# Moving the weighted values ahead of the mixing and projection steps inside each attention unit

## The chip, the cores and the metric

The kernel runs on one core of one Trainium2 chip. The metric is device microseconds of one execution, the median of several executions. A profile is one further execution, recorded by the hardware profiler. PE is the matrix engine (TensorE), with PEld its weight loads, DVE is VectorE, ACT is ScalarE, POOL is GpSimd, and SP issues most of the DMAs.

## The reference, cut to what matters

A gated transformer block on 32 sequences of 128 tokens with 128 features, everything in float32:

```
x = x + tanh(g_xattn) * xattn(layernorm(x), ctx)
x = x + tanh(g_ffn)   * ffn(layernorm(x))

xattn(x, xa):   q, k, v    = x  @ Wqkv + bqkv           16 heads of 8 features
                _, ka, va  = xa @ Wqkv_aux + bqkv_aux
                main = softmax(q k^T / sqrt(8)) v
                aux  = softmax(q ka^T / sqrt(8)) va
                out  = main * (1 - sigmoid(g)) + aux * sigmoid(g)
                return out @ Wo + bo

ffn(x):         64 experts of width 64, 8 of them for each token, out of 4 of 8 groups,
                plus one shared expert; weights are normalised sigmoid scores times 2.5
```

## The kernel before, in words

**Units.** Attention is done in 64 units: unit u is sequence b = u // 2 with kind = u % 2, kind 0 being the main attention (keys and values from x) and kind 1 the one on the context. All 16 heads of a unit are done together, as 4 groups of 32 rows of the matrix array (two heads' rows and a row that holds a constant, padded to 32).

**Steps of a unit**, each with its own function and its tiles, named as in the profile:

- `scores_max(u)`: PE computes the scores `sp` (L554, 16 matmuls on 32-row tiles of the array), DVE takes the negated maxima `nm` (L563).
- `queries(u)`: PE transposes the maxima into `nt` (L580, full array), DVE adds them to the block-wise queries and writes `qa` (L582), so that the second pass of the scores comes out with the maximum already subtracted.
- `softmax(u)`: PE computes the scores again, transposed, as `st` (L600, 32-row tiles), ACT takes the exponential into two tiles `pt` (L610).
- `values(u)`: PE multiplies `pt` with the values into `op` (L623, 32 matmuls on 32-column tiles of the array), ACT copies it to `osb` (L632). The value tile carries a column of ones, so that the sums come with it.

**Steps of a sequence**, after its second unit, in the generator `output(b, osb)`, which stops twice: `divide` transposes `osb` into `ot` (L639) and DVE divides (`rd` L642, `at` L644); `mix` adds the two kinds of attention on PE with two matmuls against the identity into `mt` (L656) and ACT copies to `msb` (L660); `project` multiplies by Wo into `yp` (L666), DVE adds it to x (L667) and takes the statistics of the second layernorm (L222).

**Steps of the next pair of sequences**, in the generator `prepare(a)`, one piece at a time: statistics, normalising on POOL, transposes `tp` (L293), projections `pp` in three pieces (L305; ACT adds the bias into `qk`, L321, and half of the masked copies `bd`, L266; POOL does the other half, L268), and the values `vp` (L349; ACT copies them with L359).

**Experts.** From the middle of attention on, groups of 128 tokens that `route` has sorted by expert group are run in between: `pair` issues gate and up products `gu` (L1026, full array, with `begin_tiles` and its transposes `xq..t`, L1004, where a new set of rows begins), `add_up` the turn `ht` (L1041) and the down product `y` (L1054; ACT scales it with L1061). When attention is over, the rest of the experts runs alone.

**Order.** The order on PE, ACT, DVE and POOL is the order of the calls: nothing is rescheduled. The loop runs over u from 0 to 68 and works on three units at a time. In iteration u, with k = u % 4:

1. `queries(u-1)`, `scores_max(u)`;
2. the first `turn`: expert products `gu`, if there are any;
3. for even k one step of `outputs` (this is `mix`), for odd k one step of `steps` (`pp` for k = 1, `vp` for k = 3);
4. `values(u-2)`, then `softmax(u-1)`;
5. in turns `add_up`, another step of `outputs` (`project` for even k, `divide` for odd k), another step of `steps`, routing.

**Banks.** Two PSUM pools serve this loop. `banks` ("s", three buffers of two banks) holds `sp`, `st`, `gu`, `ht` and the routing tiles. `bank` ("m", two buffers of one bank) holds `nt`, `mt`, `pp`, `vp`, `op`, `y`, `ot`, `yp`, `tp`, which take the two buffers in turn, so that a tile waits until the last but one before it has been read.

Of the kernel before, what the change touches and what calls it, by code (L numbers as in the profile page):

```python
# [51 lines left out]
def gated_block_kernel(  # L52
# [41 lines left out]
    def bank(name):  # L94
        return ps_m[-1].tile([P, 512], F32, tag="m", name=name)
# [155 lines left out]
    def clear_values(n):  # L251
        k = follow(nc.gpsimd.memset(vpads[n], 0.0), "POOL")
        tc.add_manual_dep(k.ins, cleared.ins.name, BEHIND)
        tv = vpads[n].rearrange("p k i g (r j) e -> p (k i g r) j e", j=2)
        for j in range(2):
            nc.gpsimd.memset(tv[:, :, j, MX + j : MX + j + 1], 1.0)
# [280 lines left out]
    def unit_parts(u):  # L537
        b, kind = divmod(u, 2)
        a, i = divmod(b, AG)
        qkk, vs, bds = parts[a]  # L540
        return b, kind, i, qkk[0], qkk[1 + kind], vs[:, kind], bds[0], bds[1 + kind]
# [32 lines left out]
    def queries(u):  # L574

        b, kind, i, q, k, v, qbd, kbd = unit_parts(u)
        nm = nm_of.pop(u)
        nt = bank(f"nt{u}")
        for n in range(4):
            nc.tensor.transpose(nt[:, ts(n, S)], nm[:, n].rearrange("p g e -> p (g e)"), ident)  # L580
        qa = work.tile([P, 2, 2, S], F32, tag="qa", name=f"qa{u}")
        V.tensor_tensor(  # L582
            qa,
            nt.rearrange("p (r j s) -> p r j s", r=2, j=2),
            qbd[:, :, :, ts(i, S)],
            ALU.add,
        )
        qa_of[u] = qa
# [26 lines left out]
    def values(u):  # L615

        b, kind, i, q, k, v, qbd, kbd = unit_parts(u)
        pt = p_of.pop(u)
        op = bank(f"op{u}").rearrange("p (n s) -> p n s", s=S)
        for r in range(2):  # L620
            for j in range(2):
                for g in range(4):
                    nc.tensor.matmul(  # L623
                        op[g * SLOT : (g + 1) * SLOT, r],
                        v[:, i, g, 2 * r + j, :],
                        pt[g // 2][:, g % 2, 2 * r + j, :],
                        start=j == 0,
                        stop=j == 1,
                    )
        if kind == 0:  # L630
            osb_of[b] = work.tile([P, 4, S], F32, tag="osb", name=f"osb{b}", bufs=1)
        nc.scalar.copy(osb_of[b][:, 2 * kind : 2 * kind + 2, :], op[:, 0:2])  # L632
        return osb_of.pop(b) if kind else None

    def divide(b, osb):

        ot = bank(f"ot{b}")
        for n in range(4):
            nc.tensor.transpose(ot[:, ts(n, S)], osb[:, n, :], ident)  # L639
        oh = ot.rearrange("p (n e) -> p n e", e=SLOT)  # L640
        rd = work.tile([P, H, 2], F32, tag="rd", name=f"rd{b}")
        V.reciprocal(rd, oh[:, :, MX : MX + 2])  # L642
        at = work.tile([P, H, 2, DH], F32, tag="at", name=f"at{b}", bufs=1)
        V.tensor_tensor(  # L644
            at,
            oh[:, :, 0:MX].rearrange("p n (j e) -> p n j e", e=DH),
            rd.unsqueeze(3).to_broadcast([P, H, 2, DH]),
            ALU.mult,
        )
        return at.rearrange("p n j e -> p (n j e)")  # L650

    def mix(b, af):

        mt = bank(f"mt{b}")
        for kind in range(2):
            nc.tensor.matmul(  # L656
                mt[:, 0:S], af[:, ts(kind, D)], ident, start=kind == 0, stop=kind == 1
            )
        msb = work.tile([P, S], F32, tag="msb", name=f"msb{b}")
        nc.scalar.copy(msb, mt[:, 0:S])  # L660
        return msb

    def project(b, msb):
        bg, i = divmod(b, BG)
        yp = bank(f"yp{b}")
        nc.tensor.matmul(yp[:, 0:D], msb, wo_sb, start=True, stop=True)  # L666
        V.tensor_tensor(x_sb[bg][:, i, :], yp[:, 0:D], x_sb[bg][:, i, :], ALU.add)  # L667
        ln_stats(x_sb[bg][:, i, :], mv2[bg][:, i, :])
# [8 lines left out]
    def scatter_some(n):  # L677

        for _ in range(min(n, len(to_scatter))):
            f, *a = to_scatter.pop(0)  # L680
            f(*a)
# [397 lines left out]
    def gather_some(n):  # L1079

        while to_gather and n:
            n -= 1
            f = to_gather.pop(0)
            while f and not f():
                f = to_gather.pop(0) if to_gather else None
# [96 lines left out]
    def round_begins():  # L1182

        nonlocal clock
        clock += 1
        if routed in (sum(ROUNDS[: c + 1]) for c in range(len(ROUNDS))):
            scatter_some(1)
        for c in range(len(ROUNDS)):
            if routed < sum(ROUNDS[: c + 1]) or to_scatter and c not in begun:
                continue  # L1190
            at = clock - begun.setdefault(c, clock)
            if at == 1:
                load_rows_of(c, 0)
            elif at >= (3 if alone else 6) and c not in started and len(parts_of) < 2:
                begin_tiles(c, 0)
                load_rows_of(c, 1)
                started[c] = clock
# [8 lines left out]
    def pair():  # L1206

        nonlocal fresh
        if todo and ready(todo[0]):
            kind, *job = todo.pop(0)  # L1210
            fresh = True
            if kind == "all":
                waiting.append((job, hidden(*job)))
            else:
                waiting.append((job, group_hidden(*job)))
                c, q, n = job
                if n == 0 and q + 1 < NQ[c]:
                    begin_tiles(c, q + 1)
                    load_rows_of(c, q + 2)
# [22 lines left out]
    NU = 2 * B  # L1242
# [23 lines left out]
    def output(b, osb):  # L1266

        at = divide(b, osb)
        yield
        msb = mix(b, at)  # L1270
        yield
        project(b, msb)
        if b % BG == BG - 1:
            routing.append(route(b // BG))

    def more(it):
        next(it, None)
# [27 lines left out]
    def turn(there):  # L1305

        if there:
            pair()
        round_begins()
        scatter_some(1)  # L1310
        gather_some(1)

    for u in range(NU + 5):
        if 10 <= u:
            for k in islice(clear, 1):
                tc.add_manual_dep(k.ins, reached[min(u, NU) - 1], AFTER)
        if 1 <= u <= len(weight_loads):
            for k in weight_loads[u - 1]():
                tc.add_manual_dep(k.ins, reached[u - 1], AFTER)
        if 0 <= u - 1 < NU:  # L1320
            queries(u - 1)
        if u == 0:
            first, steps = steps, prepare(1)
            more(steps)
            more(steps)
        if u < NU:
            scores_max(u)
        if u == 0:
            finish_gates()
            more(first)  # L1330
            ictx.close()
            rt = ctx.enter_context(tc.tile_pool(name="rt", bufs=1))
            hp = ctx.enter_context(tc.tile_pool(name="hp", bufs=2))
            clear_values(1)
            count_tables()
            nc.gpsimd.memset(lower, 1.0)
            nc.gpsimd.affine_select(
                out=lower,
                in_=lower,
                compare_op=ALU.is_gt,  # L1340
                fill=0.0,
                base=0,
                pattern=[[1, NG], [-1, NG]],
                channel_multiplier=0,
            )
        k = u % UA
        n = plan(u)

        turn(n > 0)
        if k % 2 == 0:  # L1350
            more(outputs)
        else:
            more(steps)
        osb = values(u - 2) if 0 <= u - 2 < NU else None
        if osb is not None:
            finished = output((u - 2) // 2, osb)
        if 0 <= u - 1 < NU:
            softmax(u - 1)
        add_up()
        copy_some()  # L1360
        if osb is not None:
            outputs = finished
        route_some(1)
        turn(n > 1)
        more(outputs)
        copy_some()
        route_some(2)
        add_up()
        turn(n > 2)
        if u:  # L1370
            more(steps)
        route_some(1)
        add_up()
        if k == 2 and u < NU - UA - 2:
            coming = prepare((u + 2) // UA + 1)
            more(coming)
        elif k == 3:
            more(coming)
            steps, coming = coming, iter(())
        use_bank()  # L1380
        turn(False)
        copy_some()
# [67 lines left out]
```

## Time and profile before

| | us |
|---|---|
| median of 7 executions | 1046.16 |
| lowest and highest | 1043.49, 1047.85 |
| the profiled execution, time | 1047.54 |
| the profiled execution, span | 1045.8 |

| engine | busy us | share of the span |
|---|---|---|
| PE | 942.6 | 90% |
| PEld | 638.1 | 61% |
| DVE | 608.5 | 58% |
| POOL | 539.4 | 52% |
| ACT | 494.9 | 47% |

| stretch of the span, us | what runs | PE busy us | granted PE clock |
|---|---|---|---|
| 30 to 110 | attention alone | 77.28 | 1.00 |
| 110 to 300 | attention, routing and scatters | 163.84 of 190 | 0.94 |
| 300 to 340 | the last scatters of the first round, first expert rows | 32.43 of 40 | 0.83 |
| 340 to 560 | attention with experts in between | 201.73 of 220 | 1.00 |
| 560 to 700 | experts, second round of routing | 123.84 of 140 | 0.96 |
| 700 to 950 | experts alone | 245.92 of 250 | 0.99 |
| 950 to 1046 | the last sequences through all experts, gathers | 76.00 of 96 | 0.92 |

The span is what the profiler saw of the execution; 1.74 us of the execution's own time lie around it. Busy time counts matmuls as they are issued and modelled, so the starts of neighbouring instructions tell more about the price of a step than their durations do. The granted clock is the share of full speed at which the matrix array was allowed to run.

### The profile page before, as it was taken

What the parts mean: (1) busy time and instruction counts of PE and PEld (TensorE: products, weight loads), DVE (VectorE), ACT (ScalarE), POOL (GpSimd) and SP (SyncE); (2) the same over time, 40 slices, a digit from 0 to 9 for tenths busy, and PEclk for the clock granted to TensorE, in tenths of its full rate; (3) what the DMA queues carried; (4) which work ended last, traced back from release to release, by engine and by line L of the source; (5) the groups of instructions that cost most, each with busy time, mean ns of one, the idle gap of its engine ahead of it and who ended that gap; (6) DMA issues with size and microseconds to landing.
All of it is one profiled execution on the core that took longest, in us unless ns stands there. A gap on an engine that the chain in (4) does not pass through costs nothing.

```text
span 1045.8 us, 20766 instructions
## 1 busy us (share of the span) xinstructions
PE 942.6 (90%) x7704; PEld 638.1 (61%) x7704; DVE 608.5 (58%) x1248; ACT 494.9 (47%) x943; POOL 539.4 (52%) x867
## 2 busy tenths in 40 slices
PE   6999789789897889989999799998999999999876
PEld 5777566566674566666666466665667666764332
DVE  5576875766763765575666374553455555546453
ACT  2566555454554445455544344544555555542111
POOL 3435378587676365855753767511333332007770
PEclk8999999898997999999999899999999999999989
DMA  5544234101011000100120122244222222115530
GB/s 140 141 119 144 92 131 149 41 29 44 7 42 55 22 17 24 61 19 27 39 63 12 55 81 75 78 110 110 78 84 76 76 76 69 41 50 141 141 86 25
DMA packets 100007, 75.19 MB, mean 72 GB/s; under 512 B 23942, under 2 KB 92166, under 8 KB 99910
## 3 DMA queue, kind: packets, MB, share of 16 engines
q1 hardware_dynamic: 90662, 55.11, 18.7%
q0 software_dynamic: 8960, 18.36, 5.6%
q8 instruction: 65, 1.06, 0.4%
q10 hardware_dynamic: 288, 0.39, 0.1%
q14 instruction: 32, 0.26, 0.1%
HBM read 39.63 MB, written 34.21 MB: 71 GB/s over the span
## 4 chain that ended last, share of the span: by engine, by line
PE 53%; POOL 20%; DVE 13%; issue 6%; DMA 4%; ACT 3%; SPq 1%; POOLq 0%; ACTq 0%; DVEq 0%
PE gu L1026 16%; PE y L1054 9%; POOL xslot L869 6%; POOL yg L1095 5%; PE st L600 5%; PE op L623 4%; PE ht L1041 4%; PE sp L554 3%; DVE nm L563 3%; PE pp L305 2%; POOL bd L268 2%; PE gu L970 2%; PE nt L580 2%; POOL row L234 1%; DMA xq<-xslot 1%
## 5 line engine op out<-in xcount | busy, mean ns | idle before, releaser
L954 DVE TENSOR_TENSOR th<-gu,th 128x512 f32<-128x512 f32 x158 | 108.9, 689 | 158.6 <-ACT th L947 157.0
L947 ACT ACTIVATE th<-gu 128x512 f32<-128x512 f32 (+1 forms) x132 | 78.9, 597 | 194.7 <-PE gu L1026 106.2
L563 DVE TENSOR_REDUCE nm<-sp 128x8 f32<-128x1024 f32 x128 | 150.7, 1219 | 17.2 <-PE sp L554 16.9
L1054 PEld LDWEIGHTS y<-wd_sb,hT 128*128 128x128 f32 x1008 | 130.3, 194 | 47.3 <-issue 45.7
L610 ACT ACTIVATE pt<-st 128x1024 f32<-128x1024 f32 x128 | 124.1, 1021 | 50.4 <-PE st L600 50.4
L1054 PE MATMUL y<-wd_sb,hT 128*128 x1008 | 136.8, 279 | 0.9 <-ACT hT L1043 0.9
L1026 PE MATMUL gu<-wg_sb,xqT 128*128 x252 | 133.2, 611 | 3.3 <-DVE th L954 2.7
L1095 POOL DMA_INDIRECT yg<-yslot,place x112 | 110.7, 988 | 43.4 <-issue 30.9
L1026 PE MATMUL gu<-wu_sb,xqT 128*128 x252 | 129.6, 596 | 0.0
L869 POOL DMA_INDIRECT xslot<-row,place x112 | 114.6, 1024 | 22.0 <-issue 21.0
L268 POOL TENSOR_SCALAR bd<-qk,mask 128x256 f32<-128x256 f32 x90 | 82.7, 930 | 45.1 <-ACT qk L321 44.4
L623 PE MATMUL op<-pt,v 128*32 128x128 f32 x2048 | 73.2, 286 | 24.8 <-DVE qa L582 24.3
L1006 POOL TENSOR_TENSOR wg<-xq,mine 128x256 f32<-128x256 f32 x32 | 24.6, 770 | 135.0 <-DMA xq<-xslot 134.9
L1026 PEld LDWEIGHTS gu<-wu_sb,xqT 128*128 128x128 f32 x252 | 48.2, 191 | 61.1 <-issue 61.1
L600 PE MATMUL st<-qa,qk 32*128 32x256 f32 x1024 | 82.8, 415 | 2.5 <-DVE nm L563 2.1
L554 PE MATMUL sp<-bd,qk 32*128 32x256 f32 x1024 | 80.1, 416 | 3.8 <-DVE qk L319 3.8
L1043 ACT COPY hT<-ht 128x512 f32<-128x512 f32 x126 | 74.1, 588 | 12.2 <-PE ht L1041 0.9
L623 PEld LDWEIGHTS op<-pt,v 128*32 128x32 f32 x2048 | 54.8, 114 | 39.7 <-DVE qa L582 29.3
L1041 PE MATMUL ht<-ident,h 128*128 128x128 f32 x504 | 76.1, 274 | 0.2 <-DVE th L954 0.2
L956 DVE TENSOR_TENSOR h<-th,wq 128x512 f32<-128x512 f32 x98 | 69.5, 710 | 3.3
L958 POOL TENSOR_TENSOR h<-th,wq 128x512 f32<-128x512 f32 x28 | 29.2, 1043 | 77.4 <-DVE th L954 61.1
L1061 ACT ACTIVATE yo<-y,tgf 128x128 f32<-128x128 f32 x126 | 46.4, 368 | 41.6 <-PE y L1054 33.4
(278 smaller groups left out, 1492.1 us busy)
## 6 DMA issues: line engine op xcount, KB each, us to landing
xslot<-zero SPq DMA_DIRECT2D x16, 768.0 KB, 3.8
xq<-xslot SPq DMA_DIRECT2D x32, 384.0 KB, 3.3
yslot<-yo SPq DMA_DIRECT2D x32, 256.0 KB, 2.3
cw<-w_dram SPq DMA_DIRECT2D x32, 256.0 KB, 4.0
x<-in_x_dram SPq DMA_DIRECT2D x16, 128.0 KB, 3.1
ctx<-in_ctx_dram SPq DMA_DIRECT2D x16, 128.0 KB, 2.6
wg_sb<-in_L_ffn_We_gate_dram SPq DMA_DIRECT2D x8, 256.0 KB, 3.5
wu_sb<-in_L_ffn_We_up_dram SPq DMA_DIRECT2D x8, 256.0 KB, 3.8
```

The source lines that it names most:

```text
L268: nc.gpsimd.tensor_scalar(bd[:, r, j, :], qk[:, r], mask[:, j : j + 1], None, ALU.mult)
L554: mm = nc.tensor.matmul(sp[g // 2][:, g % 2, 2 * r : 2 * r + 2, :], q[p0 : p0 + SLOT, r, ts(i, S)], kbd[p0 : p0 + SLOT, r, :, ts(i, S)], s ...
L563: V.tensor_reduce(nm[:, :, 2 * gp : 2 * gp + 2, MX].rearrange("p b g -> p g b"), sp[gp], AX.X, ALU.max, negate=True,)
L600: nc.tensor.matmul(st[g // 2][:, g % 2, 2 * r : 2 * r + 2, :], k[p0 : p0 + SLOT, r, ts(i, S)], qa[p0 : p0 + SLOT, r], start=True, stop=True,)
L610: nc.scalar.activation(pt, st[gp], AF.Exp, scale=1.0 / math.sqrt(DH))
L623: nc.tensor.matmul(op[g * SLOT : (g + 1) * SLOT, r], v[:, i, g, 2 * r + j, :], pt[g // 2][:, g % 2, 2 * r + j, :], start=j == 0, stop=j == 1,)
L869: k = nc.gpsimd.indirect_dma_start(out=xslot[c], out_offset=IndirectOffsetOnAxis(ap=place[c][:, i0 + i, r : r + 1], axis=0), in_=row[:, i, :],
L954: V.tensor_tensor(th[0:m], gu[0:m, 1], th[0:m], ALU.mult)
L1026: nc.tensor.matmul(gu[:, i], xt[:, ts(n, P)], w[:, ds(v[n], 1), :].rearrange("p o f -> p (o f)"), start=True, stop=True,)
L1041: nc.tensor.transpose(ht[:, 0, ts(p, P)], h[:, ts(p, P)], ident)
L1054: nc.tensor.matmul(y[:, 0:D], hs[:, ts(p, P)], w[:, ds(v[n], 1), p, :].rearrange("p o d -> p (o d)"), start=p == 0, stop=p == GP - 1,)
L1095: nc.gpsimd.indirect_dma_start(out=k["yg"][:, n, r, :], out_offset=None, in_=yslot[c], in_offset=IndirectOffsetOnAxis(ap=place[c][:, 2 * k ...
```

## The change

In each iteration of the loop, step 4's `values(u-2)` is called ahead of step 3 in place of behind it: the products with the values come directly behind the scores (and behind expert products, where there are any), and `mix`, `pp` or `vp` follows them. The generator `output(...)` is made at the same place as before relative to `values`; it is still handed to `outputs` only further down, so the step of `outputs` that is called here is the same one as before. Nothing else is changed, and no instruction is added or removed.

```diff
         n = plan(u)
 
         turn(n > 0)
+        osb = values(u - 2) if 0 <= u - 2 < NU else None
+        if osb is not None:
+            finished = output((u - 2) // 2, osb)
         if k % 2 == 0:
             more(outputs)
         else:
             more(steps)
-        osb = values(u - 2) if 0 <= u - 2 < NU else None
-        if osb is not None:
-            finished = output((u - 2) // 2, osb)
         if 0 <= u - 1 < NU:
             softmax(u - 1)
```

On PE the order of a unit changes from `nt sp [gu] mt|pp|vp op st` to `nt sp [gu] op mt|pp|vp st`. On ACT the copy to `osb` comes ahead of `msb`, `qk` or the values' copies; the exponentials stay behind both. The order of operations on DVE, POOL and SP stays as it was. The bank that `op` takes is now the one that was last used before `nt`, and `mt`, `pp` or `vp` takes the one of `nt`.

## Prediction

> **What bounds the kernel now.** I read the page first, then PE's timeline unit by unit, then the chain of work that ended last, in its order of time. The page says that PE is busy 90% of the span, and that the chain runs through PE for 53%, POOL 20%, DVE 13%.
>
> ```profile
> PE 942.6 (90%) x7704; PEld 638.1 (61%) x7704; DVE 608.5 (58%) x1248; ACT 494.9 (47%) x943; POOL 539.4 (52%) x867
> ...
> PE 53%; POOL 20%; DVE 13%; issue 6%; DMA 4%; ACT 3%; SPq 1%; POOLq 0%; ACTq 0%; DVEq 0%
> ...
> L623 PE MATMUL op<-pt,v 128*32 128x128 f32 x2048 | 73.2, 286 | 24.8 <-DVE qa L582 24.3
> ```
>
> The last line is the moved step, `op`: 24.3 us of PE's idle time stand in front of it, ended by DVE's `qa`. `op` does not read `qa`; it takes the bank that `nt` had, and `qa` is what reads `nt`. From the timeline, a unit without experts, one with experts, and three places where `op` has other neighbours (start, duration, in us):
>
> ```profile
> 138.30 1.15 PE L554 MATMUL sp<-bd,qk 32*128 32x256 f32 x16
> 139.37 0.71 PE L656 MATMUL mt<-ident,at 128*128 128x128 f32 x4
> 140.02 1.08 PE L623 MATMUL op<-pt,v 128*32 128x128 f32 x32
> 141.03 1.15 PE L600 MATMUL st<-qa,qk 32*128 32x256 f32 x16
> 142.10 0.49 PE L666 MATMUL yp<-wo_sb,msb 128*128 128x128 f32 x2
> ...
> 390.95 1.02 PE L1026 MATMUL gu<-wu_sb,xqT 128*128 x2
> 391.81 0.61 PE L656 MATMUL mt<-ident,at 128*128 128x128 f32 x4
> 392.34 1.08 PE L623 MATMUL op<-pt,v 128*32 128x128 f32 x32
> 393.36 1.15 PE L600 MATMUL st<-qa,qk 32*128 32x256 f32 x16
> 394.43 1.16 PE L1054 MATMUL y<-wd_sb,hT 128*128 x8
> 395.43 0.60 PE L1041 MATMUL ht<-ident,h 128*128 128x128 f32 x4
> ```
>
> ```profile
> 34.84 1.15 PE L554 MATMUL sp<-bd,qk 32*128 32x256 f32 x16
> 35.91 1.08 PE L623 MATMUL op<-pt,v 128*32 128x128 f32 x32
> ...
> 549.31 1.02 PE L1026 MATMUL gu<-wu_sb,xqT 128*128 x2
> 550.27 1.08 PE L623 MATMUL op<-pt,v 128*32 128x128 f32 x32
> ...
> 564.37 1.08 PE L623 MATMUL op<-pt,v 128*32 128x128 f32 x32
> 565.38 1.16 PE L1054 MATMUL y<-wd_sb,hT 128*128 x8
> 566.37 0.60 PE L1041 MATMUL ht<-ident,h 128*128 128x128 f32 x4
> ```
>
> The reader is to take differences of starts. The array is used in three shapes: rows (`sp`, `st`: 32*128), full (128*128), columns (`op`: 128*32). Where the shape changes, a step takes longer. `mt` takes 0.65 between rows and columns (139.37 to 140.02; 0.64 in most units), and 0.53 where a full-shape `gu` stands before it (391.81 to 392.34). `gu` takes 0.86 before `mt` and 0.96 before `op`. `y` takes 1.00 behind `st` and 0.99 behind `op`, against 0.89 where the experts run alone (575.65 to 576.54 in the timeline). So leaving a shape costs about 0.1 us and entering one another 0.1.
>
> **The change, part by part.** The same instructions run; what moves is the order and the banks. There are 64 `op` steps; in four (u = 2, 61, 63 and 65) nothing stands between, so 60 pairs are swapped: 39 without an expert product or expert transposes in between, 21 with.
>
> *39 pairs without experts: nothing.* Before: rows, full, columns, rows; after: rows, columns, full, rows; three changes of shape each way. For `mt`, before: 1.07 + 0.64 + 1.01 = 2.72 from `sp` to `st`. After: `sp` to `op` 1.07 (at 34.84), `op` to a full step 1.01 (at 564.37), and `mt` between columns and rows, which the trace does not show. It is at most the 0.64 between rows and columns, at least the 0.53 that `nt` takes before `sp` with a full step ahead of it. I take 0.64, as `y` pays the same behind `op` as behind `st`: 2.72, a difference of 0 (bounds -0.11 to 0). `pp` and `vp` go the same way.
>
> *21 pairs with experts: one change more.* Before: rows, full `gu`, full `mt`, columns, rows; three changes. After: rows, full `gu`, columns, full `mt`, rows; four. Before, from the second `gu` to `st`: 0.86 + 0.53 + 1.01 = 2.40. After: 0.96 + 1.01 + 0.64 = 2.61, with 0.53 for the last 2.50. The price is 0.10 to 0.21, and I take 0.20. The Trainium skill has a rule that speaks against this change: "TensorEngine Tiling (Array Packing)", Key Properties, says that a change of tiling mode, not of tile alone, drains the engine. It gives no time; "TensorE: Matmul & The Clock Gate" (Part 2) gives some 128 cycles for a wavefront to leave, an estimate of 0.05 us at the 2.4 GHz it states, by which one more change would cost about 1.1 us over 21 pairs.
>
> Not all 21 pay at the end. In the chain of waits, `mt|vp|pp` and `op` stand next to each other in 12 of them: at 330, 341, 383, 392, 412, 423, 432, 468, 477, 487, 508 and 520 us. In the others the chain goes through something else: the second half of `st` waits for DVE's `nm` (371, 401, 456, 497; the like at 360), or the chain leaves PE at `gu` for ACT, DVE and POOL (353, 445, 542). These I cost at nothing; if that cover goes, each is 0.2. At 330 the array runs at half clock (`op` 1.87), so 0.35. At 558 (u = 64) `op` waits for `msb`; after, `mt` waits for `osb`, and `st` comes about 0.2 later. Sum: 11 x 0.20 + 0.35 + 0.20 = 2.75 us later.
>
> *The waits for `qa`.* `op` no longer waits for it, but `mt`, `pp` or `vp` does, as it takes `nt`'s bank, and `st` does, which reads it. So what runs behind the wait is `mt` (0.64) in place of `op` (1.01): 0.37 less in even iterations; in odd ones `pp` 1.06 or `vp` 1.08: 0.05 to 0.07 more. There are 14 waits. At 119 and 148 the chain goes on through POOL, at 127, 197, 265 and in the four expert units through DVE's `nm`: nothing. At 188 the wait of 6.05 is followed by half clock and then by `yp`, on which DVE waits:
>
> ```profile
> 181.47 0.71 PE L656 MATMUL mt<-ident,at 128*128 128x128 f32 x4
> 188.24 1.93 PE L623 MATMUL op<-pt,v 128*32 128x128 f32 x32 [6.05 <-DVE qa L582]
> 190.10 2.09 PE L600 MATMUL st<-qa,qk 32*128 32x256 f32 x16
> ```
>
> `op` took 1.86 there; a cold `mt` takes 1.15 (at 249.91): 0.71 gained. At 218 (wait 3.39) the clock comes back before `yp`: 0.38 gained. At 133, 258 and 272: 0.05, 0.05 and 0.07 lost; at 286 cold `pp` against cold `op`: nothing. Together 0.92 gained.
>
> *ACT and what else is moved.* `msb` comes a step later, behind `osb` (0.37): it is ready about 0.4 us after `st` starts, and `yp` follows 1.08 after that start. `qk` (0.84) now runs while `st` does: it ends about 0.95 after `pp`, the exponentials start 1.18 after it; 0.2 are left. `osb` is earlier, so `ot` has more room. `op` now needs both exponentials at the place where `mt` stood. In the units that follow `vp`, `mt` starts only 0.20 after the second exponential ends (70.63 against 70.43), and PE starts 0.04 after a releaser (ACT's `qk`, 202.72 to 202.76): nothing. POOL's `bd` gets its `qk` 1 us later at k = 1; the copy is used three units later. If the covers on ACT went, 0.2 in some ten units would be 2 us.
>
> *Sum.* 2.75 - 0.92 = +1.8 us. The profiled execution took 1047.54 (span 1045.8), which becomes 1049.4; it stands 1.4 above the median of 1046.16, so the median becomes 1048.0.
>
> **The rivals.**
>
> *Faster, through the clock.* After waits of 6.05 (188), 3.39 (218) and 2.73 us (286) the array runs at half clock; the granted clock is 0.58 from 186 to 196. After 2.63 (127) and 2.11 (148) it does not. After the move the idle times are 5.7, 3.0 and 2.8, hardly shorter. If the clock holds all the same, `op`, `st` and their followers cost 2.9, 1.4 and 1.5 less. With 0.38 for each of two waits in place of 1.09, and 0.17 lost, that is 2.75 + 0.17 - 0.76 - 5.8 = -3.6: 1042.5. It decides from two of the three spells on. Against it: a wait of 1.62 (245) was followed by a cold spell and the same wait at 348 was not, so length alone does not set it. The Trainium skill's "TensorE: Matmul & The Clock Gate" (Part 1) puts the idle time that throttles at about 3.4 us; by it only the spell at 218 would go, and the sum would be about +0.4. This trace has one behind 2.73.
>
> *Slower by more.* All 21 expert pairs pay because the covers are thinner than the chain shows, and the waits give nothing: 19 x 0.20 + 0.35 + 0.20 + 0.17 = +4.5: 1050.7. A cold spell more (1.4 to 2.9) comes to the same. For it: the covers by `nm` are 0.4 us waits (`st` at 374, 404, 458, 500). Against it: a wait that DVE ends does not move with PE.
>
> *No change.* The later PE meets the waits for POOL's scatters (5.95 at 580, 3.49 at 317) and is swallowed: 1046.2. Against it: in both places the chain comes from PE shortly before.
>
> *The change does not do what it says* is no case here: the order after it shows `op` behind `sp` or `gu` in all 60.
>
> **How the numbers follow.** Forecast +1.8: 0.48. Slower by more: 0.20. No change: 0.18. Faster: 0.14. The range reaches from 1042.8 (the faster case; the lower bounds of the shape costs, 39 x -0.11 = -4.3, end in the same place) to 1051.5 (the slower case and some spread of the median). The likeliest case alone, with the price from 0.10 to 0.21 and 1 us of spread, is 1046.0 to 1049.5. About 0.2%, 2.1 us, is what a measurement can tell from no change, so the forecast lies close to that edge: I give half of it to each side. Slower by more than that: 0.24 + 0.19 = 0.43; faster: 0.14 and a little of the others, 0.16; within: 0.41.
>
> **What would show it.** Right: `op` at about 0.96 behind `gu` and `mt` at 1.01 behind `op` in the units from 340 to 560 us, from `gu` to `st` 2.6 in place of 2.4; units before 300 unchanged where nothing waits; the 24.3 us in front of `op` gone from it and found, slightly less, in front of `mt`, `pp`, `vp`. Wrong: `st` or `mt` starting earlier relative to `qa` than 0.6, cold spells missing or added, `op` waiting for ACT's exponentials, `yp` for `msb`.

## The result and the profile after

The changed kernel takes 1054.84 us (median of 17 runs, 1051.43 to 1058.57) against 1046.21 (44 runs of the kernel before, 1042.71 to 1049.87). The ratio is 1.0082, with a 95% interval from 1.0072 to 1.0093: 8.6 us slower, outside the predicted range. The profiled execution has a span of 1054.0 (before 1045.8).

The page of the changed kernel: busy times, the shares of the chain that ended last, and the group of the moved step.

```profile
PE 950.7 (90%) x7704; PEld 640.4 (61%) x7704; DVE 608.4 (58%) x1248; ACT 495.9 (47%) x943; POOL 540.7 (51%) x867
...
PE 53%; POOL 22%; DVE 11%; issue 6%; DMA 4%; ACT 3%; SPq 1%; POOLq 0%; ACTq 0%; DVEq 0%
...
L623 PE MATMUL op<-pt,v 128*32 128x128 f32 x2048 | 70.9, 280 | 1.3 <-ACT qk L321 1.1
```

The list of PE's waits (total us, times, longest) says where the 24.3 us went that stood in front of `op`:

```profile
PE mt L656 <- DVE qa L582: 13.8, 5, 5.7
...
PE pp L305 <- DVE qa L582: 5.7, 3, 2.4
...
PE vp L349 <- DVE qa L582: 3.6, 2, 2.2
```

Together 23.1 us: moved, and slightly less, as forecast. A unit with experts, from the timeline after:

```profile
395.51 1.02 PE L1026 MATMUL gu<-wu_sb,xqT 128*128 x2
396.46 1.08 PE L623 MATMUL op<-pt,v 128*32 128x128 f32 x32
397.47 0.71 PE L656 MATMUL mt<-ident,at 128*128 128x128 f32 x4
398.11 1.15 PE L600 MATMUL st<-qa,qk 32*128 32x256 f32 x16
```

Differences of starts: 0.95, 1.01, 0.64, so 2.60 from `gu` to `st`; 2.61 was forecast, 2.40 stood before. To see where time is lost, I subtract, for each unit, the start of its `nt` before from the one after, and look at how that shift steps from unit to unit. From unit 2 to unit 15 each step is at most 0.01 us. From there to 262 us there are steps both ways, up to 2.5 us, where the array waits or changes its clock; in all the shift goes from -1.33 at unit 15 to -0.19 at 262.04. In most of the expert units it steps by 0.17 to 0.21. The largest step is elsewhere: +3.95 between the `nt` at 262.04 and the one at 268.52 us (times of before), ahead of the first expert. There the prediction had 0.05 to 0.07 us for a wait, and nothing else.

The timeline before at that place (start, duration, engine, what it does, the wait in front of it and who ended it):

```profile
257.52 0.84 ACT L321 ACTIVATE qk<-pp,bcol 128x256 f32<-128x256 f32 x2 [1.22 <-PE pp L305]
258.11 1.83 POOL L268 TENSOR_SCALAR bd<-qk,mask 128x256 f32<-128x256 f32 x2 [2.90 <-ACT qk L321]
259.91 0.72 POOL L761 TENSOR_TENSOR eq<-eq,lower 128x256 f32<-128x256 f32 x1
260.71 0.73 POOL L762 TENSOR_TENSOR gt<-gt,eq 128x256 f32<-128x256 f32 x1
261.81 0.41 DVE L766 TENSOR_REDUCE gm<-gt 128x32 f32<-128x256 f32 x1
262.26 0.18 DVE L767 TENSOR_SCALAR gm<-gm 128x32 f32<-128x32 f32 x1
...
264.40 0.68 DVE L582 TENSOR_TENSOR qa<-nt,bd 128x512 f32<-128x512 f32 x1
265.14 1.08 PE L623 MATMUL op<-pt,v 128*32 128x128 f32 x32 [0.47 <-DVE qa L582]
266.15 1.25 PE L600 MATMUL st<-qa,qk 32*128 32x256 f32 x16
```

And after:

```profile
258.00 1.13 PE L305 MATMUL pp<-srcT,wpad 128*128 128x256 f32 x4 [2.32 <-DVE qa L582]
259.17 0.84 ACT L321 ACTIVATE qk<-pp,bcol 128x256 f32<-128x256 f32 x2 [3.05 <-PE pp L305]
259.75 1.83 POOL L268 TENSOR_SCALAR bd<-qk,mask 128x256 f32<-128x256 f32 x2 [3.77 <-ACT qk L321]
261.55 0.72 POOL L761 TENSOR_TENSOR eq<-eq,lower 128x256 f32<-128x256 f32 x1
262.35 0.72 POOL L762 TENSOR_TENSOR gt<-gt,eq 128x256 f32<-128x256 f32 x1
263.11 0.42 DVE L766 TENSOR_REDUCE gm<-gt 128x32 f32<-128x256 f32 x1 [1.41 <-POOL gt L762]
263.56 0.43 DVE L767 TENSOR_SCALAR gm<-gm 128x32 f32<-128x32 f32 x1
...
266.11 0.68 DVE L582 TENSOR_TENSOR qa<-nt,bd 128x512 f32<-128x512 f32 x1
266.85 0.88 PE L656 MATMUL mt<-ident,at 128*128 128x128 f32 x4 [1.96 <-DVE qa L582]
267.65 2.40 PE L600 MATMUL st<-qa,qk 32*128 32x256 f32 x16
```

Read it from the top. `pp` of this k = 1 unit (iteration u = 33) now stands behind the wait for `qa`, so ACT's `qk` comes 1.65 us later (257.52 to 259.17) and POOL's `bd` 1.64. POOL works in order: `eq` and `gt` of the routing, which need nothing of `bd`, are queued behind it and come 1.64 later too. DVE's `gm` had 0.37 to spare behind `gt` (its end at 261.44, `gm` at 261.81); now DVE stands still for 1.41. DVE works in order as well, and the next unit's `qa` is queued behind the routing: 1.71 later, or 1.90 against the shift of -0.19 with which the unit starts. `mt` waits for it, and then the array runs at half clock (`st` 2.40 in place of 1.25); such a stretch, with a granted clock of 0.50, is called a spell below. The windows show it (us, busy PE, PEld, DVE, ACT, POOL, then the granted clock), first before, then after:

```profile
262.00:276.00 14.00, 12.20 (x166) 9.39 (x167) 11.96 (x36) 9.21 (x20) 6.25 (x12) 1.00 0.01 2
```

```profile
262.00:276.00 14.00, 11.78 (x132) 8.63 (x132) 10.71 (x33) 6.89 (x16) 4.96 (x8) 0.76 0.01 2
```

So 1.90 of the 3.95 are the late `qa`, and the other 2.05 go with the half clock behind it.

### The profile page after: what moved, and what is told of

Its sections match the earlier page's. It is cut to its first block, busy times and chain, and to the rows that moved or that the text cites. A ratio compares the mean times of both kernels' runs of the same rounds, so it can differ in the third digit from the quotient of the medians.

```text
span 1054.0 us, 20745 instructions
## 1 busy us (share of the span) xinstructions
PE 950.7 (90%) x7704; PEld 640.4 (61%) x7704; DVE 608.4 (58%) x1248; ACT 495.9 (47%) x943; POOL 540.7 (51%) x867
## 4 chain that ended last, share of the span: by engine, by line
PE 53%; POOL 22%; DVE 11%; issue 6%; DMA 4%; ACT 3%; SPq 1%; POOLq 0%; ACTq 0%; DVEq 0%
PE gu L1026 16%; PE y L1054 8%; POOL xslot L869 7%; POOL yg L1095 5%; PE st L600 5%; PE ht L1041 4%; PE sp L554 4%; PE op L623 3%; DVE nm L563 2%; PE pp L305 2%; POOL bd L268 2%; PE nt L580 2%; PE gu L970 2%; PE mt L656 1%; POOL row L234 1%
## 5 line engine op out<-in xcount | busy, mean ns | idle before, releaser
L623 PE MATMUL op<-pt,v 128*32 128x128 f32 x2048 | 70.9, 280 | 1.3 <-ACT qk L321 1.1
```

The costliest lines, as they stand in the source:

```text
L623: nc.tensor.matmul(op[g * SLOT : (g + 1) * SLOT, r], v[:, i, g, 2 * r + j, :], pt[g // 2][:, g % 2, 2 * r + j, :], start=j == 0, stop=j == 1,)
```

## The experiments

Three theories. **A, shapes:** the one more change of shape in each of 21 expert units. **B, POOL's queue:** the late `bd` holds up the routing, and through DVE `qa` and PE. **C, spells:** the stretches of half clock fall wherever the order happens to put them, and the loss has no one place. Ratios are to the kernel before on the same chip, with their 95% interval; a ratio times 1046.4 gives us. Two groups of runs were made on chips on which the kernel before takes 1078.4 us, at a mean granted clock of 0.949 in place of 0.962 (`e_late33`, `e_late1729`, `e_lateplain`, `after_again`), and 1074.7 us (`e_late_b`, `e_lateplain_b`, `e_evenplain_b`, `e_k3`); for these only ratios are given. On the others it takes 1046.4 to 1046.8.

### Which units

The edits, shortened:

```diff
-        osb = values(u - 2) ...      # always ahead of mix, pp, vp
+        first_values = n > 0         # e_expert; n == 0: e_plain; k % 2 == 0: e_even; k == 1: e_k1
+        if first_values: values(u - 2) ahead of mix, pp, vp, else behind
```

Only expert units (`e_expert`):

> The values come ahead of mix, pp or vp only in the 21 units that have expert products or expert transposes in between; the other 39 keep the order of before. Theory A (one more change of array shape in each of these units) expects the steps of +0.19 to +0.21 that the changed kernel shows per unit from 340 us on, so +2.0 to +2.8 us in all, about 1049. Theory B (the late qk of a k = 1 unit holds up POOL's bd, behind it the routing's eq and gt, then DVE and so qa) has its places at 127, 218 and 260 us, all ahead of the first expert, so it expects the same +2.0 to +2.8 here. Theory C (any shift of the order moves the spells of half clock about, wherever they fall) expects something outside of that, from -3 to +6, with spells that are new behind 340 us.

Measured: 1051.00, 1.0033 (1.0018 to 1.0048): +3.5, with 1.9 to 5.0. The steps in its profile are those of A: units 43 to 63 show 0.19 to 0.21 where the change applies. On top came a spell at 442 us, 1.65 by the shift, and a longer one at 719 us (6.8 us at half clock in place of 3.4), where nothing was changed.

Only units without experts (`e_plain`):

> The values come ahead of mix, pp or vp only in the 39 units with nothing of the experts in between. Theory B expects most of the loss here: the changed kernel's +8.6 less the 2.0 to 2.8 of the experts, so +5.5 to +6.5, about 1052. Theory A expects nothing, 1046. Theory C expects a loss of any size, and not at k = 1 in particular.

Measured: 1053.23, 1.0055 (1.0032 to 1.0079): +5.8. So most of the loss isn't shapes, and the two parts add to 9.3, near the 8.6.

Only even k (`e_even`):

> The values come first only where k is even, that is ahead of mix; pp and vp stay ahead of the values as before. Theory B expects the losses at 127, 218 and 260 us to be gone, as they are at k = 1, and the gains at 188 and 245 us (1.3 and 2.5 us, k = 0) to stay; with about 2 us for the shape in some ten expert units that is -2 to +1, 1044 to 1047. Theory C expects about half of the changed kernel's loss, +4, with no such split. Theory A alone: +1.2.

Measured: 1046.63, 1.0002 (0.9989 to 1.0016): the loss is gone without the odd units, as B expects.

Only k = 1 (`e_k1`):

> The values come first only where k = 1, so that the second piece of pp, with ACT's qk and POOL's bd behind it, is the only thing that comes later (16 units). Theory B expects +5 to +8.5 (1051 to 1055): three places of +1.5 us at 127, 218 and 260 us, a cold spell of some 4 us behind the last, and 0.2 for each of about five expert units. Theory A alone: +1. Theory C: a quarter of the loss, +2, or any sign.

Measured: 1048.31, 1.0016 (1.0000 to 1.0033): +1.7, a miss for B's number. The profile shows why. `gm` waits the same 1.41 for `gt` (at 264.54 in its own time), and the step there is +1.90: the whole late `qa`, but no half clock.

```profile
265.24 0.71 PE L656 MATMUL mt<-ident,at 128*128 128x128 f32 x4 [0.26 <-ACT qk L321]
268.28 1.08 PE L623 MATMUL op<-pt,v 128*32 128x128 f32 x32 [2.32 <-DVE qa L582]
269.29 1.25 PE L600 MATMUL st<-qa,qk 32*128 32x256 f32 x16
```

A wait of 2.32 in front of `op` left the clock alone here; one of 1.96 in front of `mt` in the changed kernel did not. All seven profiles in which `qa` is late there and the even unit behind it is changed too have the spell. That it takes both edits isn't shown all the same: the longer wait happens to fall across two windows of the clock, as the last section shows, and this is one profile.

### POOL's queue

The masked copies are issued at three places of an iteration. The first is left out, so that a k = 1 unit's `bd` goes to the second, behind a step of the routing. On PE and DVE nothing changes its place, on ACT one activation; on POOL `bd` comes behind `eq` and `gt` at u = 33 and at one later place, and behind one more scatter at u = 17 and 29 (and at one place late in attention).

```diff
         add_up()
-        copy_some()
         if osb is not None:
             outputs = finished
         route_some(1)
```

On the changed kernel (`e_late`):

> The changed kernel, with the first of the three places where the masked copies are issued left out, so that a k = 1 unit's copies go out half a unit later: on POOL bd comes behind the routing's eq and gt at 260 us and at one place later on, and behind one more scatter at 127 and 218 us; on ACT its half of the copies comes later as well. No other order changes. Theory B (POOL waits for qk in bd, and the routing behind it is late) expects the wait of gm for gt at 263 us (1.41) to go, qa there to come 1.4 to 1.7 earlier, the cold spell at 268 to 275 to go with it, and the time to fall by 2 to 5, to 1050 to 1053. Theory C (spells fall anywhere) expects 1054.8 within 1.5. If bd's lateness then delays the scores of the next pair, it becomes slower; the copies are used three units later, so none is expected.

Measured: 1046.54, 1.0004 (0.9992 to 1.0017). The whole loss is gone, more than was expected. On the kernel before, the control (`b_late`):

> The same edit (the first place of the masked copies left out) on the kernel before. Its control: in the kernel before qk comes ahead of the values, POOL's bd waits less, and gm does not wait for gt at 260 us. Theory B expects 1046.4 within 1.5; if it falls as much as the changed kernel does with the same edit, the copies' place is worth something whatever the order of the values, and theory B has no support from the pair.

Measured: 1047.11, 1.0011 (0.9994 to 1.0028). The copies' place by itself shows no gain in the time, and the pair speaks for B against C. In the profiles it does have an effect without the values ahead: at the "one later place", u = 45, the kernel before already has `bd` ahead of `eq` and `gt`, and `gm` waits for it. First before, then `b_late`:

```profile
368.28 0.42 DVE L766 TENSOR_REDUCE gm<-gt 128x32 f32<-128x256 f32 x1 [2.46 <-POOL gt L762]
```

```profile
365.12 0.42 DVE L766 TENSOR_REDUCE gm<-gt 128x32 f32<-128x256 f32 x1 [0.64 <-POOL gt L762]
```

In all five profiles with all copies late the unit behind it comes 1.81 to 1.83 us earlier, and one at 109 us 0.8. That can be why `e_late` gains more than was expected. In `b_late` it doesn't reach the time; its runs have a mean granted clock of 0.958, against 0.962 before.

All but k = 3 (`e_not3`):

> The changed order in all units but those with k = 3, which keep vp ahead of the values. In the changed kernel's profile the k = 3 units lose nothing ahead of the experts, and even units alone gave 1046.6, k = 1 alone 1048.3. If the parts add, even and k = 1 together give 1046.4 + 0.2 + 1.9 = 1048.5 and k = 3 alone has to hold the other 6. If instead they act together (k = 1 makes qa late, and in the k = 2 unit behind it mt stands behind that wait with nothing left to run), this kernel gives 1053 to 1055. Theory B with the second reading: 1054. Theory C: anything between.

Measured: 1051.56 (6 runs), 1.0051 (1.0033 to 1.0069). It is more than the parts (the sum of `e_even` and `e_k1` would be 1.0018), but about 3 us are missing to the changed kernel.

One place alone, `if u != 33: copy_some()` (`e_late33`):

> The changed kernel with the copies half a unit later in one unit only, u = 33 (260 us), where POOL's bd then comes behind the routing's eq and gt; every other unit is as in the changed kernel. In the profiles the two units there cost the changed kernel 1.57 + 3.95 and nothing with all copies late. Theory B with that one place as its main cost expects 1054.8 less 4 to 5.5: 1049.3 to 1050.8. Theory C (the late copies helped because they moved spells of half clock all over) expects less than 2 of the 8.3 here.

Measured: 1.0022 (1.0004 to 1.0040). Against 1.0082, or 1.0070 in the repeat below, this one `bd` is worth 0.0048 to 0.0060, some 5 to 6 us, with intervals that leave 2 to 8. Its profile has the place as in the kernel before: `eq` and `gt` ahead of `bd`, no wait in front of `gm`, and none left in front of `mt`.

```profile
262.13 0.71 POOL L761 TENSOR_TENSOR eq<-eq,lower 128x256 f32<-128x256 f32 x1 [2.92 <-DVE eq L759]
262.92 0.72 POOL L762 TENSOR_TENSOR gt<-gt,eq 128x256 f32<-128x256 f32 x1
264.44 1.83 POOL L268 TENSOR_SCALAR bd<-qk,mask 128x256 f32<-128x256 f32 x2 [0.79 <-ACT qk L321]
266.32 0.41 DVE L766 TENSOR_REDUCE gm<-gt 128x32 f32<-128x256 f32 x1
266.76 0.18 DVE L767 TENSOR_SCALAR gm<-gm 128x32 f32<-128x32 f32 x1
...
268.90 0.68 DVE L582 TENSOR_TENSOR qa<-nt,bd 128x512 f32<-128x512 f32 x1
269.64 0.71 PE L656 MATMUL mt<-ident,at 128*128 128x128 f32 x4
270.28 1.62 PE L600 MATMUL st<-qa,qk 32*128 32x256 f32 x16
```

The two other places, `if u not in (17, 29): copy_some()` (`e_late1729`), and the changed kernel once more for a second profile (`after_again`):

> The changed kernel with the copies half a unit later at u = 17 and u = 29 only (127 and 218 us), where POOL's bd then comes behind one more scatter. The profiles show steps of +0.4 + 1.6 and +0.2 + 1.45 there in the changed kernel, nothing with all copies late. Theory B expects 1054.8 less 2 to 3.5: 1051.3 to 1052.8, and together with the u = 33 kernel the whole 8.3 of the late copies. Theory C expects no change beyond 1.5.

> The changed kernel once more, for a second profile of the same program. Theory B expects the same waits: gm for gt 1.41 us at about 263 us, qa late, mt waiting about 2 for it, and the steps of about +1.6 and +2 to +4 there. Theory C expects the spells of half clock at 126, 268, 352 and 544 us to lie elsewhere; those that come back at the same place belong to the order and not to chance.

Measured: 1.0051 (1.0027 to 1.0075) for the first, one time of 1.0069 for the second. The ratio seemed to give u = 17 and 29 some 3 us; the profiles did not: their steps at 29 are +1.66 and +0.92, and the step of +3.95 is in both. So both were timed on one chip (`after_b`, `e_late1729_b`):

> The changed kernel, timed beside the next one on the same chip. 1.0072 to 1.0093 of the kernel before, as at first.

> The copies late at u = 17 and 29 only. If bd ahead of a scatter costs something there, 2 to 3.5 us below the changed kernel of the same chip. If u = 33 is the one place that counts, as the profiles have it (the step of +3.95 is the same with and without this edit, and the steps at u = 17 and 29 come and go from run to run), the same as the changed kernel within 1.5.

Measured: 1.0070 (1.0045 to 1.0096) and 1.0059 (1.0036 to 1.0083): 0.8 us apart, no difference that can be told. The scatters at u = 17 and 29 aren't shown to cost anything; u = 33 is the place that counts.

The steps of the shift at two places, from each kernel's profile, in us:

| kernel | behind u = 33 (262 to 268) | 350 to 356 |
|---|---|---|
| changed, three profiles | +3.95, +3.95, +3.01 | +1.79, +1.79, +1.85 |
| late at u = 17, 29, two profiles | +3.95, +3.54 | +1.79, +1.86 |
| without experts only | +3.54 | +1.67 |
| all but k = 3 | +3.54 | +0.21 |
| k = 1 only | +1.90 | +0.01 |
| even only | -0.01 | +0.20 |
| late at u = 33 | -0.01 | +0.20 |
| all copies late, two profiles | 0.00, -0.01 | +0.21, +0.21 |
| all late, without experts only, two profiles | 0.00, 0.00 | +1.60, 0.00 |
| even without experts, two profiles | +0.01, 0.00 | +0.01, +1.59 |
| k = 3 only | +0.11 | +0.01 |
| experts only; before with late copies | -0.01; 0.00 | +0.21; +0.01 |

The first column is B without exception: every kernel in which `bd` stands late ahead of `eq` pays 1.9 to 3.95 there, none other pays more than 0.11. In the second, 0.20 is the change of shape and 1.6 a spell at 352 us. All five profiles in the first two rows have it, and so do single profiles of kernels whose `bd` isn't late; the last section shows what decides. With it or with the width of the intervals, the 3 to 4 us that the profiles show behind u = 33 become the 5 to 6 us that the times show.

### What is left, and a faster version

Two versions leave the expert units as they were. `n == 0` together with late copies is `e_lateplain`; `k % 2 == 0 and n == 0` with the copies at their old place is `e_evenplain`.

> The values first only in units with even k and without experts in between: the even kernel without its expert units, where it paid 0.19 to 0.21 about ten times. Theory A expects 1046.6 less 2, 1044.6, and this is the version that could beat the kernel before. Theory C expects no such step: 1046.6 within 2.

Measured: 1044.81, 0.9983 (0.9972 to 0.9993): 1.8 us faster than the kernel before.

> The changed order with all copies late, but the values ahead of mix, pp and vp only in the 39 units with nothing of the experts in between. Theory A and B together expect the late copies' 1046.5 less the shape changes of the 21 expert units, 2 to 3 by their steps in the profiles: 1043.5 to 1044.5, below the kernel before and level with the even units alone. If the expert units cost what the kernel that moved only them showed (3.5 to 4.6), 1042 to 1043. Theory C expects 1046.5 within 2.

Measured: 0.9976 (0.9949 to 1.0003). For the expert units' price the three were set side by side, with k = 3 alone (`e_k3`):

> The copies-late kernel once more, for a comparison on one chip with the next two. Theory B and A: 1.000 of the kernel before (its first ratio was 1.0004, from 0.9992 to 1.0017): +2.75 of the expert units set against a gain of as much in the waits for qa.

> Copies late, and the changed order only in the 39 units without experts. Theory A (0.20 for each of the expert units that are on the path) expects 2.0 to 2.8 us below the copies-late kernel of the same chip, so 0.9975 of the kernel before. If the expert units cost more than their shape changes, 3.5 to 4.6 below. If spells of half clock decide, no difference.

> The changed order only in even units without experts, copies at their old place. If odd units cost nothing once POOL's copies are late, this stands level with the previous kernel, within 1 us, at 0.9975 to 0.9985. If pp ahead of the values has a worth of its own, this is faster than that kernel by more than 1.

> The changed order only in units with k = 3, where vp comes behind the values. No copies for POOL hang on vp, so theory B expects nothing but the shape changes of about five expert units: +0.6 to +1.0. If k = 3 holds the 3 us by which even and k = 1 together fall short of the changed kernel: +3.

Measured: 1.0012 (0.9990 to 1.0034), 0.9980 (0.9956 to 1.0003), 0.9984 (0.9965 to 1.0002) and 1.0017 (0.9993 to 1.0040). The expert units cost 0.0032, 3.3 us at 1046; their steps give 2.3, and the medians' intervals allow either. The two faster versions agree within 1 us and with their first runs. Each of their four ratios lies 1.7 to 2.5 us below the kernel before; one of the four intervals excludes no change, the first of `e_evenplain`. What k = 3 costs (+1.8, with -0.7 to +4.2) stays unclear, and with it the 3 us that `e_not3` lacks.

## Why the prediction was wrong, point by point

**The step that failed** is, in its words, "POOL's `bd` gets its `qk` 1 us later at k = 1; the copy is used three units later." The prediction's sum has no term for it. Two things were wrong in it. The delay was 1.65 and not 1, since `pp` now also stands behind a wait for `qa` that it used to run ahead of. And the reader of `bd` was looked at, not the queue behind `bd`: at u = 33 two operations of the routing stood there, DVE's next with 0.37 us to spare, and behind DVE's routing the `qa` that PE waits for. The trace of before held all of it: the four rows from `bd` to `gm` are enough. In place of nothing it cost 3 to 4 us by the profiles and 5 to 6 by the times, of 8.6.

**The shapes** were right in mechanism and size: 0.95, 1.01 and 0.64 for 0.96, 1.01 and 0.64, steps of 0.19 to 0.21. Between the `nt` at 337 and the one at 547 us the profile's steps without spells add up to 2.3, with two units gaining 0.2 back; the sum had 11 x 0.20 there. At 330 us, where it had 0.35, the steps of three profiles are -0.36, +0.14 and -0.30. Forecast 2.75 in all; timed, 3.3, with intervals that hold both. The Trainium skill's rule on changes of mode ("TensorEngine Tiling (Array Packing)", Key Properties) was right in sign, and the prediction's estimate of 0.05 us for one change a quarter of the 0.20 measured.

**The 39 units without experts** cost nothing where nothing waits: units 2 to 15 step by 0.01 at most.

**The waits for `qa`** moved as said, but the 0.92 did not come as forecast. At 188 us `mt` behind the wait runs 1.15 in place of `op`'s 1.86, and the shift steps by -1.29 and -0.73 in two profiles (the third, on a slower chip, loses 6 us just ahead of it); it also steps by -0.46 in `e_expert`, which has the old order there, so 0.3 to 0.8 are the change's. At 218 the predicted gain of 0.38 is a loss of 0.20, with a longer spell behind it. Moving only the even units without experts does gain, 1.8 us, more than the 0.92; its first profile gives 1.35 of that to a spell at 286 us that is gone there, but the second, `e_evenplain_b`, has that spell, so where the gain arises stays open.

**The rivals.** "A cold spell more" was named as a way to the slower case and priced at 1.4 to 2.9; that it came and cost 2.05 was right. It had no place, and that a late `qa` would bring it was not seen. The faster case through the clock did not come: from 35 to 560 us the array is at half clock for 47.8 us in place of 37.5, and for 37.5 in `after_b`.

**What would show it wrong** had "cold spells missing or added", which was what happened, and nothing about POOL or DVE.

## What to carry to other kernels

An instruction that is moved behind a wait delays not only its reader: what is queued behind that reader on its engine is late as well, and so on from engine to engine. List for each engine what stands behind the late instruction, and how much slack the first reader of that has. Where a copy that nobody needs soon stands ahead of work that somebody does, put it behind. Look first at the few places where two engines' queues meet, here two units of 64 in which the routing and a k = 1 copy fall together (u = 33, and u = 45, which stalls in both kernels), and not at the mean of all units.

## What the runs showed of the hardware that was not expected

Spells of half clock don't go by the length of the wait alone: 1.96 us brought one (the granted clock over 14 us was 0.76), 2.32 us at the same place in `e_k1` did not. In every trace the granted clock changes only at the edges of windows of 3.41 us, whose position differs from profile to profile, and what counts is how busy PE was in the window just before. First the changed kernel, whose wait lies in one window (PE busy 1.46 of 3.42), then `e_k1`, whose wait is cut by an edge (1.92 and 2.32):

```profile
263.87:267.29 3.42, 1.46 (x35) 1.20 (x36) 3.25 (x12) 1.05 (x3) 1.46 (x2) 1.00 0.00 0
267.29:270.70 3.41, 3.41 (x22) 2.54 (x21) 2.60 (x8) 1.19 (x3) 0.00 (x0) 0.50 0.00 0
```

```profile
263.77:267.18 3.41, 1.92 (x22) 1.24 (x20) 2.46 (x9) 2.48 (x7) 2.56 (x3) 1.00 0.02 5
267.18:270.60 3.42, 2.32 (x49) 1.79 (x50) 3.39 (x7) 0.51 (x2) 0.00 (x0) 1.00 0.00 0
270.60:274.01 3.41, 3.41 (x32) 2.61 (x33) 2.36 (x13) 3.33 (x6) 0.72 (x1) 1.00 0.00 0
```

Over all twenty traces (25 to 1020 us, windows at full clock): half clock follows each of the 190 windows in which PE was busy less than 40%, 84 of the 317 with 40 to 70%, and 2 of the 4241 with 70% or more. The spell at 352 us goes the same way. A wait of 1.6 us stands there in the kernel before too; where one window holds 1.22 us or more of it the spell comes, where an edge leaves 1.10 at most it doesn't. Some spells come back: the one behind u = 33 is in all three profiles of the changed kernel. Others don't: the spell at 127 to 134 us is in the first of the three profiles alone. The Trainium skill's "TensorE: Matmul & The Clock Gate" (Part 1, What's actually happening) says that the gate watches a free-running window, so that runs of one kernel differ; that agrees with the windows and with the spells that come and go. Its throttling after an idle window of some 3.4 us doesn't fit as a rule on idle time: a window with PE busy for 43% was enough here.

Some of DVE's small operations slow down beside POOL. The same `gm` (L767, 128x32) takes 0.18 us at 262.26 before, with POOL idle, and 0.43 at 263.56 after, with POOL's `bd` running since 263.49. Over all traces, L767 and L769 take 0.18 in each of 204 cases with POOL idle, and 0.18 to 0.43 in 116 beside a running POOL operation; of the 1.90 by which `qa` is late, 0.4 arise between `gm` and `qa` in this way. The Trainium skill's "SBUF — State Buffer" (Who interferes with whom) names a pair of ports that VectorE and GpSimd share under an exclusive lock. The sign agrees; the size doesn't: `bd` runs for 0.92 at a time, `gm` lost 0.25 and had ended before it. That the ports are the cause isn't shown.
